# Layer 0's q, k and v of a two-layer masked-attention kernel: tokens stationary and 384 columns moving instead of 128

## Chip, cores and metric

The kernel runs on one core of a Trainium2 chip, in fp32 throughout. The time is the device time of one execution in microseconds (us); below it is the median of the runs shown. A profile is one further execution, recorded instruction by instruction. PE is TensorE (PEld its weight loads), DVE VectorE, ACT ScalarE, POOL GpSimd, and SP is the engine whose queue issues the DMAs here.

## What is computed

128 graphs of 128 nodes with 512 features each go through two layers of masked attention. Both layers use the same adjacency mask; layer 1 adds the diagonal to it. Cut to what matters (`norm` is a layer norm over the features, without gains unless named):

```python
def layer0(x):                                  # 4 heads of 64
    q, k, v = x @ Wq, x @ Wk, x @ Wv            # 512 -> 256 each
    sim = where(adj, q @ k.T * 64 ** -0.5, -max)
    return softmax(sim) @ v @ Wo + bo           # per head, then 256 -> 512
def layer1(x):                                  # 8 heads of 64
    q, k, v = split((norm(x) * gamma + beta) @ w_qkv.T)   # 512 -> 3 x 512
    sim = where(adj | eye, q @ k.T * 64 ** -0.5, -1e9)
    return softmax(sim) @ v @ w_out.T + b_out
x = norm(x + layer0(x)); x = norm(x + layer1(x))
```

## The kernel before

**Groups and steps.** Two graphs make a group, so there are 64 groups of 256 tokens. The kernel is a software pipeline written out by hand: `opening()` handles the first groups, `step(s)` runs for s from 2 to 63, and two closing functions and `last()` drain it. In one step layer 0's q, k, v are made for group s, layer 0's scores for group s - 1, layer 0's attention output for group s - 2, and layer 1 runs three to five groups behind. Nothing reorders the instructions: the order of the calls in `step` is the order of each engine's queue, and an engine that waits holds up everything behind it on its own queue. All DMAs go through SP's queue in the same way.

**Products.** Every large product (layer 0's q, k, v at L460, layer 1's q, k and v at L338, both output projections at L498) is made by a seven-product scheme on 2 x 2 blocks instead of eight. The two rows of blocks are the two graphs, the sums of blocks of the input (`xs`, `so`) are formed by POOL at L302, and those of the weights are formed once. Each of the seven products is taken out of PSUM by ACT or DVE (L469, L471, L474). A matmul holds one operand of 128 columns in the array (stationary) and streams the other (moving).

**Layer 0's products, the lines changed.** In `product_0` (L438) each of the seven products is six matmuls of 128 moving columns: for q and k the weights are stationary and the tokens move, so they come out with features on partitions, as the scores want them; for v the tokens are stationary. Two of the six belong to each of q, k and v, one for each half of that block's features. The three results lie side by side in one PSUM bank as 384 columns and are taken out together into `qkv0`. v's slot in `qkv0` alternates between the two ends with the group's parity, because the attention of group s - 2 is still to read it.

**x with features on partitions.** The products need x turned. Groups 0 to 2 are turned by PE (`transposed`, L239, matmuls L245, copies L246). Later groups go through DRAM: `load_ahead` loads x with tokens on partitions, `turn` has DVE transpose 32 x 32 blocks (L229) and writes them to a DRAM scratch (`put`, L214), `arrive` fetches them with the block rows moved to the right partitions in four DMAs of 32 partitions each (`fetch`, L220), and `in_order` has ACT copy them into place (L256). Layer 1's input, its q and k, and all probabilities go through DRAM in the same way, with the same helpers and the same scratch tile `turned` (two buffers).

**Order around the change.** `product_0(s, 4)` is followed by layer 1's q, k products; then come the third part's normalisation (DVE's reciprocal L588, POOL's multiplication L589), its block transposition (L607) and the fetch of the first two parts' probabilities. At the end of a step ACT orders layer 1's q (L412); the next step begins with the scores (L531 for layer 0, L536 for layer 1).

Of the kernel before, what the change touches and what calls it, by code (L numbers as in the profile page):

```python
# [10 lines left out]
F32 = mybir.dt.float32  # L11
# [6 lines left out]
P = 128  # L18
D = 64
G = 2  # L20
# [7 lines left out]
def kernel(ctx: ExitStack, tc: tile.TileContext, x, adj, wq, wk, wv, wo, bo,  # L28
# [45 lines left out]

    X = {}

# [10 lines left out]
    def load(g):  # L87
        load_rows(g)
        load_mask(g)

    def load_ahead(g):
        if g < NG:
            X[0] = one.tile([P, G, E], F32, tag="x", name=f"x_{g}")
            nc.sync.dma_start(X[0], x[g * G:(g + 1) * G].rearrange("b n e -> n b e"))
            load_mask(g)

    R[0] = five.tile([P, G, E], F32, tag="r", name="r_0")
    M[0] = six.tile([P, G, N], U8, tag="m", name="m_0")
    for b in range(G):
        nc.sync.dma_start(R[0][:, b], x[b])  # L100

# [9 lines left out]
    HF = INNER[0] // 2  # L111
    w0 = const.tile([P, KC, 2, 3, HF], F32, name="w0")
    ws0 = const.tile([P, 3, KC // 2, 3, HF], F32, name="ws0")
    for h in range(2):
        for i, w in enumerate((wq, wk, wv)):
            nc.sync.dma_start(w0[:, :, h, i, :], w[:, h * HF:(h + 1) * HF].rearrange("(c p) f -> p c f", p=P))
    nc.sync.dma_start(M[0], adj[:G].rearrange("b i j -> i b j"))
    load(1)
# [4 lines left out]
    bias1 = const.tile([P, E], F32, name="bias1")  # L123
    nc.sync.dma_start(bias1, b_out[None, :].to_broadcast([P, E]))

    w1 = const.tile([P, KC, 3 * INNER[1]], F32, name="w1")
# [60 lines left out]
    def weight_sums_0():  # L187
        combine(*(w0[:, c:c + KH, h].rearrange("p c t f -> p c (t f)") for c in (0, KH) for h in range(2)),
                *(ws0[:, i].rearrange("p c t f -> p c (t f)") for i in range(3)))

# [14 lines left out]
    WO = (wo0, wo1)  # L205
    RATIO, XT, V = {}, {}, {}
    qkv0 = const.tile([P, G, 2, 4, P], F32, name="qkv0")
# [3 lines left out]
    def put(t, name):  # L211

        scr = dram.tile(list(t.shape), F32, tag=name.split("_")[0], name=name)
        nc.sync.dma_start(scr, t)  # L214
        return scr
# [7 lines left out]

    def turn(l, g):
        if not 0 <= g < NG:
            return
        t = one.tile([P, 4, G * KC * 32], F32, tag="turned", bufs=2, name=f"turned{l}_{g}")
        for b in range(G):
            nc.vector.transpose(t.rearrange("p a (b c i) -> p a b c i", b=G, c=KC)[:, :, b],  # L229
                                (R[g] if l else X[0])[:, b].rearrange("p (c a i) -> p a c i", a=4, i=32))  # L230
        SCR[l] = put(t, f"scr{l}_{g}")

    def arrive(l, g):
        if not 0 <= g < NG:
            return
        RAW[l] = one.tile([P, 4, G, KC, 32], F32, tag=("raw0", "raw")[l], name=f"raw{l}_{g}")
        fetch(RAW[l].rearrange("p a b c i -> p a (b c i)"), SCR[l])

    def transposed(g):  # L239

        xT = XT[0, g] = one.tile([P, KC, T], F32, tag="xT0", name=f"xT0_{g}")
        for b in range(G):
            pt = mm_tile(f"xt{g}_{b}")
            for c in range(KC):
                nc.tensor.transpose(pt[:, c * N:(c + 1) * N], R[g][:, b, c * P:(c + 1) * P], ident)  # L245
            (nc.scalar.copy, nc.vector.tensor_copy)[b](xT[:, :, b * N:(b + 1) * N],  # L246
                                                       pt.rearrange("p (c n) -> p c n", c=KC))
        sums(0, g)

    def in_order(g):  # L250

        if not 0 <= g < NG:
            return
        xT = XT[0, g] = one.tile([P, KC, T], F32, tag="xT0", name=f"xT0_{g}")
        for b in range(G):
            nc.scalar.copy(xT[:, :, b * N:(b + 1) * N].rearrange("p c (a j) -> p a c j", a=4),  # L256
                           RAW[0][:, :, b])

# [108 lines left out]
    def taken_tokens(g, i, src):  # L367

        if i in (1, 5, 6):
            return tap("qk", g, i, src)  # L370
        if i == 4:
            done = src
        else:
            done = EV["qk", {2: 1, 3: 6, 7: 5}[i]]
            nc.vector.tensor_add(done, src, done)
        what, b = {2: ("k", 0), 7: ("q", 1), 3: ("q", 0), 4: ("k", 1)}[i]
        if i in (2, 7):
            TQ[what] = one.tile([P, 4, G, K1 * 32], F32, tag={"k": "xT0", "q": "raw"}[what],
                                name=f"t{what}_{g}")
            SCRQ[what] = dram.tile([P, 4, G, K1 * 32], F32, tag=f"scr{what}", name=f"scr{what}_{g}")  # L380
        t = TQ[what][:, :, b]
        nc.vector.transpose(t.rearrange("p q (c j) -> p q c j", j=32),
                            done.rearrange("p (c q j) -> p q c j", q=4, j=32))
        if what == "k":
            nc.sync.dma_start(SCRQ[what][:, :, b], t)
        elif i == 3:
            nc.sync.dma_start(SCRQ[what], TQ[what])
# [50 lines left out]
    def product_0(g, *which):  # L438
# [3 lines left out]
        xT = XT[0, g].rearrange("p (h c) (b n) -> p b h c n", h=2, b=2)  # L442
        xs = XS[0, g]
        for i in which:
            left = {1: xT[:, 0, 0], 2: xT[:, 0, 1], 3: xs[:, 3], 4: xT[:, 1, 1], 5: xs[:, 0],
                    6: xs[:, 1], 7: xs[:, 2]}[i]
            right = {1: w0[:, :KH, 0], 2: w0[:, KH:, 0], 3: w0[:, KH:, 1], 4: ws0[:, 2],
                     5: w0[:, :KH, 1], 6: ws0[:, 0], 7: ws0[:, 1]}[i]
            bank, first = INTO[i]
# [4 lines left out]
            acc = ACC[0, bank]  # L454
            odd = g % 2
            todo = [(t, c) for t in range(3) for c in range(KH)]
            for n, (t, c) in enumerate(todo):
                lhsT, rhs = (right[:, c, t], left[:, c]) if t < 2 else (left[:, c], right[:, c, t])
                at = (t + odd) % 3
                nc.tensor.matmul(acc[:, at * P:(at + 1) * P], lhsT, rhs, start=first and n == 0,  # L460
                                 stop=n == len(todo) - 1, skip_group_check=True)
            src = acc[:, :3 * P]
# [51 lines left out]
    def scores(s, *parts):  # L514

        made = {}
        for part in parts or PARTS:
# [8 lines left out]
            if part == 0:  # L526
                for b in range(G):
                    for h in range(HEADS[0]):
                        r = slice((h % 2) * D, (h % 2 + 1) * D)
                        q_, k_ = (qkv0[r, b, h // 2, i, :] for i in (1, 2))  # L530
                        nc.tensor.matmul(ps[h % 2][:, b * K0 + h // 2, :], q_, k_, start=True, stop=True)  # L531
            else:
                b = part - 1
                for h in range(HEADS[1]):
                    r = slice((h % 2) * D, (h % 2 + 1) * D)
                    nc.tensor.matmul(ps[h % 2][:, h // 2, :].rearrange("p (a j) -> p a j", j=32),  # L536
                                     QO[g, b][r, h // 2], keys_of(g, b, h // 2, r), start=True, stop=True)
# [245 lines left out]
    def opening():  # L783

        transposed(0)
        cleared(1, 0)

        for h in range(2):
            nc.scalar.activation(w0[:, :, h, 0, :], w0[:, :, h, 0, :], AF.Copy, scale=SCALE)
        product_0(0, 1)  # L790
# [6 lines left out]
        product_0(0, 4)  # L797
        transposed(1)

        made = scores(1)  # L800
# [17 lines left out]
        product_0(1, 4)  # L818
        transposed(2)

    def step(s):
# [3 lines left out]
        if s > 3:  # L825
            in_order(s)
            sums(0, s)
            arrive(1, s - 3)
        flush()
        load_rows(s - 1)  # L830
        masked(made, s, 0, 1, 2)
        if s == 3:
            turn(1, s - 3)
            arrive(1, s - 3)
        attend(s)
# [16 lines left out]
        stats(0, s - 2, 0)  # L852
        if s == 2:
            turn(0, s + 1)
            arrive(0, s + 1)
        product_0(s, 6)
# [14 lines left out]
        if s == 3:  # L871
            weight_sums(w1qk, wsqk, 1)
        if s > 2:
            turn(0, s + 1)
        product_0(s, 4)
        if s in (2, 3):
            prepare(len(setup) - (s == 2))
        normalised(s, 2)
        qk(s - 3, 1)
        if s == 2:  # L880
            prepare(1)
            in_order(s + 1)
        flush()
        if s > 2:
            probs_arrive(s, 0, 1)
        qk(s - 3, 2)
        blocks(s, 2)
        qk(s - 3, 6)
# [14 lines left out]
        probs_arrive(s, 2)  # L903
        if s > 2:
            arrive(0, s + 1)
        out_product(1, s - 5, 1, 2)
# [6 lines left out]
        if s > 2:  # L913
            turn(1, s - 2)
        cleared(s + 1, 0, 1, 2)
# [3 lines left out]
        out_product(1, s - 5, 7, 3, 4)  # L919
        q_in_order(s - 3)  # L920
        addend(0, s - 1)
        v(s - 3, 7)
# [6 lines left out]
        if s == NG - 1:  # L929
            arrive(1, s - 2)  # L930
            addend(1, s - 4)
# [186 lines left out]
```

## Time and profile before

| What | Value |
|---|---|
| Median of three runs (lowest to highest) | 2762.74 us (2762.73 to 2763.69) |
| The profiled execution's own time | 2765.02 us |
| Its span, first to last instruction | 2763.2 us |
| Granted PE clock, mean | 0.999 |
| PE matmul records | 18353, of which 5376 at L460 |
| DMA: bytes, mean rate | 561.42 MB, 203 GB/s |
| DMA packets' share of 16 engines | 72.0% |

The span leaves out what lies around the instructions, so it is a little under its own execution's time. In the profile's lines the parts are: line of the code, engine, operation, out<-in by the program's names, sizes; x gives the count, and in brackets stands the idle time before and what ended it. A matmul's duration there reaches from its start to the modelled end of its drain, and successive matmuls overlap. "SPq" is SP's queue issuing a DMA; the transfer itself goes on after it.

### The profile page before, as it was taken

The page shows a single profiled execution, that of the slowest core. Times are in us where ns is not written, and L with a number is a line of the kernel's source. Part 1 is how long each engine was busy: PE and PEld are TensorE (multiplying, and loading weights), DVE is VectorE, ACT ScalarE, POOL GpSimd, SP SyncE. Part 2 cuts the span into 40 slices and gives each one's busy share as a digit, 9 for nine tenths or more (in the row PEclk, how much of TensorE's full clock was granted, in tenths as well). Part 3 has the DMA queues.
Part 4 walks back from the last instruction along what each step waited for, and adds up shares of the span by engine and source line. Part 5 has one row for each costly group of instructions (what it writes and reads, how often), then busy time and mean ns, then how long its engine had stood idle before and what let it go on. Part 6 is the DMA issues. An engine that isn't in the chain of part 4 may idle for free.

```text
span 2763.2 us, 53794 instructions
## 1 busy us (share of the span) xinstructions
PE 2742.5 (99%) x18353; PEld 2180.1 (79%) x18353; DVE 1948.0 (70%) x3537; ACT 1526.8 (55%) x4869; POOL 1749.0 (63%) x2311
## 2 busy tenths in 40 slices
PE   9999999999999999999999999999999999999998
PEld 8978778778787787787777877877878778778787
DVE  5777677677677776776777767767767777677664
ACT  4456465465564564655655646546556455465554
POOL 5566666666666666666666666666666666666664
PEclk9999999999999999999999999999999999999999
DMA  5567877777778778777777787777777777877741
GB/s 171 154 201 208 222 209 210 215 209 213 215 208 219 209 206 227 206 211 213 209 221 207 206 224 207 210 216 208 215 214 208 217 211 207 223 208 212 196 118 62
DMA packets 473760, 561.42 MB, mean 203 GB/s; under 512 B 52104, under 2 KB 366992, under 8 KB 473488
## 3 DMA queue, kind: packets, MB, share of 16 engines
q1 hardware_dynamic: 473488, 557.99, 72.0%
q8 instruction: 147, 2.41, 0.4%
q14 instruction: 125, 1.02, 0.1%
HBM read 299.37 MB, written 258.47 MB: 202 GB/s over the span
## 4 chain that ended last, share of the span: by engine, by line
PE 97%; DMA 1%; POOL 1%; ACT 1%; DVE 1%; issue 0%; SPq 0%; POOLq 0%; ACTq 0%; DVEq 0%
PE qka L338 16%; PE a L460 13%; PE oa L498 12%; PE qkf L338 8%; PE va L338 8%; PE av L659 6%; PE f L460 6%; PE of L498 6%; PE qkc L338 4%; PE vf L338 4%; PE c L460 3%; PE oc L498 3%; PE sc L531 2%; PE sc L536 2%; PE vc L338 2%; PE sc_a L536 2%
## 5 line engine op out<-in xcount | busy, mean ns | idle before, releaser
L580 ACT ACTIVATE sm<-sm,nmax 128x128 f32<-128x128 f32 x1536 | 595.9, 395 | 7.0 <-DVE nmax L571 5.3
L589 POOL TENSOR_TENSOR sm<-sm,rec 128x1024 f32<-128x1024 f32 x192 | 364.1, 1896 | 292.9 <-DVE rec L588 292.9
L681 POOL TENSOR_TENSOR r<-r,bias 128x1024 f32<-128x1024 f32 x128 | 301.4, 2356 | 139.6 <-ACT r L680 139.6
L502 DVE TENSOR_TENSOR r<-oa,r 128x256 f32<-128x256 f32 x508 | 212.3, 418 | 170.1 <-PE oa L498 138.3
L580 ACT ACTIVATION_READ_ACCUMULATOR sm<-sm,nmax 128x1 f32 x1536 | 298.1, 194 | 0.0
L348 ACT COPY ev<-va 128x256 f32<-128x256 f32 x128 | 47.7, 372 | 438.3 <-PE va L338 438.2
L700 POOL TENSOR_SCALAR ve<-mv 128x2 f32<-128x2 f32 x191 | 41.4, 217 | 372.8 <-DVE mv L693 362.3
L607 DVE STREAM_TRANSPOSE turnedp<-sm 128x1024 f32<-128x1024 f32 x188 | 233.4, 1242 | 48.6 <-POOL sm L589 43.8
L302 POOL TENSOR_TENSOR xs<-xT 128x256 f32<-128x256 f32 x256 | 187.9, 734 | 111.0 <-ACT xT L256 91.1
L571 DVE TENSOR_REDUCE nmax<-sm 128x8 f32<-128x1024 f32 x192 | 226.2, 1203 | 0.1
L338 PE MATMUL qka<-wsqk,xs 128*128 128x512 f32 x472 | 221.8, 592 | 0.0
L338 PE MATMUL qkf<-w,xs 128*128 128x512 f32 x472 | 221.8, 592 | 0.0
L498 PE MATMUL oa<-wso,so 128*128 128x256 f32 x760 | 206.3, 380 | 2.1 <-POOL so L302 1.8
L498 PE MATMUL of<-wo,so 128*128 128x256 f32 x760 | 206.1, 380 | 0.8 <-POOL so L302 0.4
L726 ACT ACTIVATE r<-r,shift,root 128x512 f32<-128x512 f32 x254 | 192.6, 807 | 0.6 <-POOL shift L715 0.6
L565 DVE COPY_PREDICATED sm<-m,sc 128x512 f32<-128x512 uint8 x256 | 172.8, 728 | 12.2 <-PE sc L531 3.3
L338 PEld LDWEIGHTS qkf<-w,xs 128*128 128x128 f32 x472 | 89.7, 190 | 112.9 <-issue 112.9
L338 PEld LDWEIGHTS qka<-wsqk,xs 128*128 128x128 f32 x472 | 89.7, 190 | 112.9 <-issue 98.8
L692 DVE BATCH_NORM_STATS2 st<-r 128x6 f32<-128x512 f32 x254 | 174.9, 689 | 2.3
L551 POOL MEMSET sm<- 128x1024 f32 x192 | 174.9, 952 | 0.0
L498 PEld LDWEIGHTS of<-wo,so 128*128 128x128 f32 x760 | 143.7, 190 | 22.0 <-POOL so L302 2.1
L302 POOL TENSOR_TENSOR so<-aT 128x256 f32<-128x256 f32 (+1 forms) x254 | 150.5, 592 | 4.4 <-ACT aT L664 2.3
(182 smaller groups left out, 6788.7 us busy)
## 6 DMA issues: line engine op xcount, KB each, us to landing
scrp<-turnedp SPq DMA_DIRECT2D x188, 512.0 KB, 3.2
pT<-scrp SPq DMA_DIRECT2D x252, 256.0 KB, 4.8
scr<-turned SPq DMA_DIRECT2D x123, 512.0 KB, 3.0
raw<-scr SPq DMA_DIRECT2D x492, 128.0 KB, 3.9
r<-in_x_dram SPq DMA_DIRECT2D x63, 512.0 KB, 3.8
out_dram<-r SPq DMA_DIRECT2D x63, 512.0 KB, 3.5
pT<-scrp SPq DMA_DIRECT2D x248, 128.0 KB, 4.1
x<-in_x_dram SPq DMA_DIRECT2D x61, 512.0 KB, 5.8
```

Of the source, the lines that this page charges most:

```text
L302: nc.gpsimd.tensor_tensor(o, a0, a1, op=op)
L338: nc.tensor.matmul(o, lhsT, rhs, start=first and m == 0, stop=m == len(todo) - 1, skip_group_check=True)
L460: nc.tensor.matmul(acc[:, at * P:(at + 1) * P], lhsT, rhs, start=first and n == 0, stop=n == len(todo) - 1, skip_group_check=True)
L498: nc.tensor.matmul(acc, left[:, c], right[:, c], start=first and c == 0, stop=c == hk - 1, skip_group_check=True)
L502: nc.vector.tensor_add(part, acc, part)
L551: nc.gpsimd.memset(sm, NEG1 if part else NEG0)
L571: nc.vector.tensor_reduce(NMAX[part], SM[part], AX.X, ALU.max, negate=True)
L580: nc.scalar.activation(sm[:, i, k, :], sm[:, i, k, :], AF.Exp, bias=nmax[:, i, k:k + 1], accum_out=total[:, i, k:k + 1])
L589: nc.gpsimd.tensor_tensor(SM[part], SM[part], rec[:, :, :, None].to_broadcast([P, 2, K1, N]), op=ALU.mult)
L607: nc.vector.transpose(t.rearrange("p q (h r) -> p q h r", r=32), SM.pop(part).rearrange("p i k (q r) -> p q (i k) r", r=32))
L681: nc.gpsimd.tensor_tensor(R[g], R[g], (bias0, bias1)[l][:, None, :].to_broadcast([P, G, E]), op=ALU.add)
L726: nc.scalar.activation(R[g][:, b], R[g][:, b], AF.Identity, bias=shift[:, b:b + 1], scale=root[:, b:b + 1])
```

## The change

For groups from 3 on, the tokens are stationary for q and k too, and the weights of q, k and v move together: 384 columns in a matmul for even groups; for odd groups, where v lies at the other end, 256 for q and k and 128 for v. The weights' layout in `w0` changes so that q, k and v of one half are one access. q and k then come out with tokens on partitions, and are turned through DRAM (`turn_qk0`, `arrive_qk0`); the keys are read by the scores straight from the fetched tile, in pieces of 32, and q is put in order by one ACT copy (`q0_in_order`). Groups 0, 1 and 2 (`PLAIN_0`) keep the six narrow matmuls.

x is no longer turned through DRAM, nor by PE. `load_quarters` loads it so that features 128a to 128a + 127 of token 32m + j lie on partition 32a + j; one block transposition by DVE, in two instructions, then gives x with features on partitions. The features' order over the partitions changes with it, so the weights of layer 0 are loaded in the same order, in four DMAs each, those of wq from ACT's queue. x as rows is loaded separately for all groups. Layer 1's k gets a scratch tile of its own, one graph at a time, since it shared one with the turned x.

```diff
+    def load_quarters(g):
+        X[0] = one.tile([P, BB, E // 4], F32, tag="x", name=f"x_{g}")
+        src = x[g * G:(g + 1) * G].rearrange("b (m j) (a f) -> a j (b m) f", j=32, a=4)
+        for a in range(4):
+            nc.sync.dma_start(X[0][32 * a:32 * a + 32], src[a])
     def load_ahead(g):
         if g < NG:
-            X[0] = one.tile([P, G, E], F32, tag="x", name=f"x_{g}")
-            nc.sync.dma_start(X[0], x[g * G:(g + 1) * G].rearrange("b n e -> n b e"))
+            load_quarters(g)
             load_mask(g)
+    def transposed(g):
+        xT = XT[0, g] = one.tile([P, KC, T], F32, tag="xT0", name=f"xT0_{g}")
+        half = BB // 2
+        for m in (slice(0, half), slice(half, BB)):
+            nc.vector.transpose(xT.rearrange("p c (m j) -> p m c j", j=32)[:, m],
+                                X[0][:, m].rearrange("p m (c i) -> p m c i", i=32))
+    load_quarters(0)
...
-    w0 = const.tile([P, KC, 2, 3, HF], F32, name="w0")
+    w0 = const.tile([P, KC, 3, 2, HF], F32, name="w0")
-    for h in range(2):
-        for i, w in enumerate((wq, wk, wv)):
-            nc.sync.dma_start(w0[:, :, h, i, :], w[:, h * HF:(h + 1) * HF].rearrange("(c p) f -> p c f", p=P))
+    for i, w in enumerate((wq, wk, wv)):
+        for a in range(4):
+            (nc.sync if i else nc.scalar).dma_start(
+                w0[32 * a:32 * a + 32, :, i].rearrange("p c h f -> p c (h f)"),
+                w[a * P:(a + 1) * P].rearrange("(c i) f -> i c f", i=32))
+    load_mask(0)
+    load_rows(0)
     load(1)
...
+    transposed(0)
+    load_quarters(1)
...
+    def turn_qk0(g):
+        if not 0 <= g < NG or g in PLAIN_0:
+            return
+        t = one.tile([P, 4, 2, 4, 32], F32, tag="turned", bufs=2, name=f"turnedqk_{g}")
+        for i in range(2):
+            nc.vector.transpose(t[:, :, i], qkv0.rearrange("p b h t (q j) -> p q t (b h) j", j=32)[:, :, 1 + i])
+        SCR[0] = put(t.rearrange("p q t m j -> p q (t m j)"), f"scrqk_{g}")
+    def arrive_qk0(g):
+        if 0 <= g < NG and g not in PLAIN_0:
+            RAW[0] = one.tile([P, 4, 2, 4, 32], F32, tag="raw0", name=f"rawqk_{g}")
+            fetch(RAW[0].rearrange("p a t m j -> p a (t m j)"), SCR[0])
+    def q0_in_order(g):
+        if 0 <= g < NG and g not in PLAIN_0:
+            nc.scalar.copy(qkv0.rearrange("p b h t (a j) -> p t (b h) a j", j=32)[:, 1],
+                           RAW[0][:, :, 0].rearrange("p a m j -> p m a j"))
...
-            todo = [(t, c) for t in range(3) for c in range(KH)]
+            elif odd:
+                todo = [(parts[:, lo:hi], left[:, c], right[:, c, t0:t1])
+                        for lo, hi, t0, t1 in ((1, 3, 0, 2), (0, 1, 2, 3)) for c in range(KH)]
+            else:
+                todo = [(parts, left[:, c], right[:, c]) for c in range(KH)]
...
     def opening():
-        transposed(0)
+        sums(0, 0)
...
     def step(s):
         if s > 3:
-            in_order(s)
             sums(0, s)
-            arrive(1, s - 3)
+            arrive(s - 3)
...
-        if s > 2:
-            turn(0, s + 1)
         product_0(s, 4)
+        transposed(s + 1)
+        turn_qk0(s)
...
         qk(s - 3, 2)
+        arrive_qk0(s)
         blocks(s, 2)
...
         probs_arrive(s, 2)
-        if s > 2:
-            arrive(0, s + 1)
...
         q_in_order(s - 3)
+        q0_in_order(s)
```

In `opening`, `transposed(1)` is followed by `load_quarters(2)` and the sums; step 2's own calls of `turn(0, 3)`, `arrive(0, 3)` and `in_order(3)` are gone.

## The prediction

> **What bounds the kernel now.** I read the page's busy shares first, then the shares of the chain that ended last.
>
> ```profile
> PE 2742.5 (99%) x18353; PEld 2180.1 (79%) x18353; DVE 1948.0 (70%) x3537; ACT 1526.8 (55%) x4869; POOL 1749.0 (63%) x2311
> PE 97%; DMA 1%; POOL 1%; ACT 1%; DVE 1%; issue 0%; SPq 0%; POOLq 0%; ACTq 0%; DVEq 0%
> ```
>
> PE is both the busy engine and the path. A busy PE proves little by itself, so I looked for its gaps: between the scores of consecutive groups the trace has 42.35 us in 56 of the 58 steps from 5 to 62, and the chain in order of time is PE piece after piece without a hole. So the price of a matmul is its place in that chain, not the mean duration of its record (a 128-wide record lasts 275 ns, but the next starts after 112). Lines of the chain (start, length, piece), steady state and opening:
>
> ```profile
> 1237.80 1.34 PE c L460 x12
> 1239.13 0.43 PE oa L498 x2
> 1247.56 1.72 PE qka L338 x4
> ...
> 72.25 1.79 PE qka L338 x16
> ```
>
> Every fp32 matmul stands as two records ("passes"): the code asks for 42 x 64 = 2688 matmuls at L460, the trace has 5376 records. A pass moving 128 columns costs 1.34/12 = 111.6 ns (means of the starts: 111.5 to 111.7), 256 columns 215.8, 512 columns 1.717/4 = 429.2. The last two lie on a line, 0.8336 ns a column plus 2.4 ns; 128 lies 2.5 ns above it. The last line is a control in this kernel: the plain qk products of early groups do the same arithmetic in 16 narrow passes, 1.79 us where 4 wide ones take 1.72.
>
> **What the skill says.** "TensorE: Matmul & The Clock Gate", section "Back-to-back issue gap", lists 134, 262 and 518 cycles for N of 128, 256, 512: a constant per matmul, so wider is cheaper per column. This trace agrees in form (one fp32 pass takes twice the column time, then 2.4 ns, 4.9 at 128). "VectorE: DVE Perf Modes", section "The three transpose paths": the DVE transposes only 32x32 blocks. That is why a full turn needs a DRAM trip here, and why loading feature quarters onto partition quarters can spare it; a 128x512 block transpose takes 0.68 to 0.71 us in this trace. "DMA: Bandwidth & Descriptors", section "Issuing engines are not separate DMA queues": moving wq's loads to ACT saves issue time, not bandwidth. No run here shows loads issued by ACT yet.
>
> **The change, part by part.**
>
> *Products.* For groups 3 to 63 a product's 12 narrow passes become 4 of 384 columns (30 even groups), or 4 of 256 and 4 of 128 (31 odd ones, since v stays in the other slot). No row has 384 columns: the line gives 0.8336 x 384 + 2.4 = 322.5 ns; bounds are 320.0 (no constant) and 325.0 (the constant of 128), and at worst three narrow passes, 334.8. I take 322.5. Even: 7 x (12 x 111.6 - 4 x 322.5) = 7 x (1339 - 1290) = 0.344 us. Odd: 7 x (1339 - (863 + 446)) = 0.207 us. Sum 30 x 0.344 + 31 x 0.207 = 10.3 + 6.4 = **16.7 us**, all on the path; from 384 and from the odd narrow passes (109.1 on the line to 114) come -4.2 to +4.2. That w0 is now read in three pieces of 128 I cost at nothing: keys in four pieces of 32 (L536) go 16 passes in 0.89 us, and the same form takes over layer 0's scores, now L531.
>
> *x.* The turn of x through DRAM goes (2 transposes, 1 put, 4 fetches, 2 ACT copies of 0.617). In its place 4 loads of 128 KB, and 2 transposes of the same size, later by one product in DVE's order. *q, k.* Added: 2 DVE transposes (2 x 0.70), 1 put, 4 fetches, 1 ACT copy (0.62). Per step DVE +1.4 us, ACT -0.6, SP +3 issues; the sums of x on POOL no longer wait for ACT's copies at the step's start (91 us of POOL idle in all, none of it on the path). Where they land decides; DVE, ACT and SP at one step's handover:
>
> ```profile
> 1204.94 0.52 DVE L474 TENSOR_TENSOR qkv<-f,e 128x384 f32<-128x384 f32 x1
> 1205.38 1.28 DVE L229 STREAM_TRANSPOSE turned<-x 128x512 f32<-128x512 f32 x2
> 1206.59 0.16 DVE L588 RECIPROCAL rec<-total 128x8 f32<-128x8 f32 x1
> 1208.75 0.69 DVE L375 TENSOR_TENSOR eqk<-qkc,eqk 128x512 f32<-128x512 f32 x1 [2.00 <-PE qkc L338]
> ...
> 1206.37 0.46 ACT L471 COPY qkv<-a 128x384 f32<-128x384 f32 x1
> ...
> 1206.69 0.34 SPq L214 DMA_DIRECT2D scr<-turned  x1
> 1208.32 1.78 SPq L220 DMA_DIRECT2D pT<-scrp  x4
> 1210.21 0.52 SPq L385 DMA_DIRECT2D scrk<-tk  x1
> 1211.54 0.52 SPq L611 DMA_DIRECT2D scrp<-turnedp  x1
> ```
>
> New wait 1: x's transposes wait for product 4's reads of xT0, which end about 1205.3 (qk starts 1205.2): DVE comes free just then, cost nothing. New wait 2: the q, k transposes wait for ACT's copy of product 4, 1206.83; they end about 1208.3. Queued behind them on DVE are the reciprocal (1206.6 to about 1208.4) and the first qk addition, which waited 2.00 us for PE anyway. The reciprocal's reader on POOL started at 1208.34 behind sums: 0.2 us late, absorbed before its transposition at 1210.27. New wait 3: k's two halves now share one tile, so the second half's transposition (1217.27) waits for the first half's put, issued by 1210.6 and landed 3.4 later: 1214.0, cost nothing. **So the DVE's 2.0 us hole is the cover; without it 1.4 us a step would be exposed.**
>
> SP: the put moves from 1206.7 to 1208.4, the four pT fetches and the k put slip 0.4, and the new fetches wait for the put to land (3.0 us median), until 1211.4, and are issued by 1213.2. Behind them the third part's put slips from 1211.5 to 1213.2. SP then has nothing until 1217. Later it saves the x fetches (1.85 us) and pays three more x loads (1.2). In bandwidth the fetches move from the step's end into 1211 to 1217, where the engines are full; the free time there (1216.5 to 1217.7, 1220) takes all but some 0.8 us, so q's landing slips 0.8. ACT then runs q's copies at about 1225.2 and the new one by 1227.1; the next scores stand at 1229.2. Slack 2 us: cost nothing. x's 512-byte packets take 27 ns, 1024 a group, against 84 for 256 of 2 KB: 1.7 instead of 1.3 us of 16 engines, or 2.4 if loads to 32 partitions run as slowly as the fetches do (218 GB/s). Off the path.
>
> *Opening.* This is the only place where DMA is on the path:
>
> ```profile
> 4.74 5.33 DMA w<-in_L_gnn_Wv_dram
> 10.38 5.69 DMA raw_r<-in_L_gnn_w_qkv_dram
> 16.12 0.67 PE w_qkvt L144 x4
> 21.08 0.87 PE xt L245 x8
> 36.98 0.87 PE xt L245 x8
> ```
>
> PE waits at 16.1 for the first rows of w_qkv; the DMA engines are full from 2 to 28 us (298, then 364 GB/s). Ahead of these rows now come x of group 0 once more (as rows) and x of group 1 in quarters: 1 MB, at 300 to 364 GB/s 2.9 to 3.5 us; SP has 9 more issues ahead at about 0.5 us, 4.5 us, less the waits it had. Weights in wider packets give some back. I take +3.0 us (1 to 5). Back come PE's transposes for groups 1 and 2, 0.87 each; but they covered the scores' wait for ACT's copy of product 4, which then shows about 0.55: 0.3 each. Those of group 0 gave way to 1.4 us of DVE before the first product, inside the same wait for weights. Net **+2.4 us** (-0.5 to +5).
>
> **Sum.** 2763.2 (span; the profiled execution itself took 2765.02) - 16.7 + 2.4 = 2748.9. The median of the runs shown, 2762.74, is 0.5 under that span; the same difference gives 2748.4. I say **2748.5**.
>
> **Rivals.**
> 1. *Forecast*, chance 0.74: 2748.5, own range 2742 to 2755 (-4.2 and -2.9; +4.2 and +2.6).
> 2. *The opening gives instead of takes* (weights land sooner in wider packets, rows are not waited for), 0.08: -16.7 - 3 or more, about 2742.
> 3. *Width pays nothing at 384* (three pieces cost three passes, 334.8): even groups 0, odd 6.4, opening +2.4: 2758.7. Against it speaks the line through 256 and 512. Chance 0.05; or a stall of some 0.2 us a step with the same result, 0.02.
> 4. *A small stall in every step*, some 0.1 us from DVE's fuller handover: 61 x 0.1 = 6.1, 2754.6. Chance 0.05.
> 5. *Slower*: q's way through DRAM becomes the bound. The copy of layer 0's q stands on ACT behind layer 1's q copies (1.15), which wait for fetches queued behind all new traffic; scores of the next step, first on PE, wait for it. For it: those fetches were already just in time (ACT waited for them in 12 of 59 groups), and DMA is full there. Against it: slack. It decides once q's landing slips over 2.6 us instead of 0.8; at 3.4 us each step stalls 0.8, 61 x 0.8 = 49, less 14: about 2797. Chance 0.06.
>
> **Numbers.** A change within 0.2% (5.5 us) cannot be told from none. Faster: cases 1, 2, 4, 0.87; same: case 3, 0.07; slower: case 5, 0.06. Range 2741 to 2757: it takes in both bounds of the 384-wide pass and of the opening, cases 2 and 4.
>
> **What would show it.** Right: steps of 42.01 us (even) and 42.14 us (odd) where 42.35 stood; L460 pieces of 1.29 and 1.31 us; no L245; the first w_qkvt near 19 us; DVE near 72%, its wait for qkc gone from 2.0 to some 0.3. Wrong: PE idle before L531 with ACT's q copy or a DMA as its releaser (case 5), PE waiting for a bank that DVE reads late at the qk products (case 4), 384-wide passes near 335 (case 3).

## The result, and the profile after

| | median, us | lowest to highest | ratio to before (95% interval) |
|---|---|---|---|
| before, 12 runs | 2762.93 | 2762.37 to 2764.33 | |
| changed, 12 runs | 2763.99 | 2759.03 to 2765.92 | 1.0003 (0.9994 to 1.0012) |

No difference that can be measured; the forecast was 14 us faster. The changed kernel's times also spread over 6.9 us where the other's spread over 2.0. Its profiled execution was its fastest, 2759.03 us (span 2757.3), so a second one was profiled as well (own time 2764.44, span 2762.7), which is nearer to the median. The busy shares and the shares of the chain that ended last, in the first:

```profile
PE 2725.2 (99%) x15781; PEld 2024.6 (73%) x15781; DVE 2025.0 (73%) x3662; ACT 1510.6 (55%) x4805; POOL 1750.2 (63%) x2311
PE 89%; DMA 4%; ACT 3%; DVE 1%; POOL 1%; SPq 1%; issue 1%; ACTq 0%; POOLq 0%; DVEq 0%
```

PE is as busy in share as before, but its part of the chain fell from 97% to 89%: 11% of the path now runs through other things, DMA first. In the second execution it is 84%, with 6% DMA. What the matmuls themselves did is read from the chain (start, length, piece), group s odd, then even:

```profile
1238.07 1.31 PE c L490 x8
...
1280.19 1.29 PE c L490 x4
```

These answer to 1.34 us for 12 narrow passes before, and are the 1.31 and 1.29 that were forecast. Steps that nothing disturbs take 42.00 us (even) and 42.14 us (odd) where 42.35 stood. So the width pays in full; the time is lost elsewhere. Three lines of the list of waits (engine and line waiting, what for: us in total, times, longest) lead there:

```profile
ACT qo L435 <- DMA rawq<-scrq: 133.8, 59, 3.6
DVE eqk L396 <- PE qkc L359: 20.2, 59, 0.4
DVE tk L405 <- DMA scrk<-tk: 19.4, 22, 1.7
```

The middle one is DVE's hole in every step, 115.6 us in all before and now 20.2: it is filled by the new transpositions, as costed. The other two are DMAs. ACT's wait for layer 1's fetched q was 4.1 us in 12 steps before and is now in every step; DVE's wait at the k transposition for its own previous put did not exist. One step in the chain in order of time (step 13) shows the second of these at work:

```profile
490.49 1.30 DVE turnedqk L267 x2
...
491.88 0.28 SPq L234
...
494.57 7.34 DMA scrk<-tk
...
502.00 0.73 DVE tk L405
...
502.78 1.13 PE va L359 x4
```

The new transpositions (L267) and the issue of the new put (L234) stand ahead on the chain. The put of k's first half is issued at 494.57 and lands 7.34 us later. Only then may DVE overwrite the tile with the second half (it had been free for 1.51 us by then), and PE's product `va`, which needs the bank that DVE was to empty, starts 0.32 us late. SP's queue in the same step (start, length of the issue):

```profile
492.33 2.14 SPq L240 DMA_DIRECT2D pT<-scrp  x4
494.57 0.52 SPq L408 DMA_DIRECT2D scrk<-tk  x1
495.13 2.16 SPq L240 DMA_DIRECT2D rawqk<-scrqk  x4
497.74 0.52 SPq L643 DMA_DIRECT2D scrp<-turnedp  x1
500.52 0.34 SPq L410 DMA_DIRECT2D scrq<-tq  x1
502.75 0.52 SPq L408 DMA_DIRECT2D scrk<-tk  x1
506.09 1.73 SPq L240 DMA_DIRECT2D rawq<-scrq  x4
```

The k put is issued right behind a fetch of four DMAs that stood there before as well. The new fetch of four more follows it, and the q put comes behind that. The fetch of q, which waits for its put, follows 5.6 us after the put's issue.

**Where the time went.** Steps are counted from one group's layer 0 scores to the next. Against a second profile of the kernel before (own time 2763.11, span 2761.3; the experiments tell why not the first), the second profile of the changed one gives:

| Stretch | Forecast, us | Measured, us |
|---|---|---|
| Width: steps 5 to 62 at 42.00 and 42.14 instead of 42.35 | -16.0 | -16.4 |
| What these steps take above 42.00 and 42.14 | 0 | +11.4 |
| Opening, up to the scores of step 5 | +1.85 | +4.5 |
| Last step before the closing | -0.2 | +0.2 |
| Closing, from the last layer 0 scores to the end | 0 | +1.65 |
| Sum | -14.3 | +1.4 |

The forecast's 16.7 us of width were for 61 steps. 58 of them have 16.0; those of steps 3 and 4 (0.55) are taken off the opening's +2.4 here, that of step 63 (0.2) stands in the last step. The spans differ by 1.4 too. In the first profile of the changed kernel the second line is 6.5 us: the stalls are what varies from execution to execution. Set side by side, the steps of one profile lose time on PE at two places only: at the products `va` and `vc` 4.9 us in the first profile and 6.8 in the second, in 10 or 11 steps, and at the next step's scores and the product right behind them 1.7 and 4.6.

### The profile page after: what moved, and what is told of

The parts are those of the page before. It is cut to its first block, busy times and chain, and to the rows that moved or that the text cites. A ratio compares the mean times of both kernels' runs of the same rounds, so it can differ in the third digit from the quotient of the medians.

```text
span 2757.3 us, 49223 instructions
## 1 busy us (share of the span) xinstructions
PE 2725.2 (99%) x15781; PEld 2024.6 (73%) x15781; DVE 2025.0 (73%) x3662; ACT 1510.6 (55%) x4805; POOL 1750.2 (63%) x2311
## 4 chain that ended last, share of the span: by engine, by line
PE 89%; DMA 4%; ACT 3%; DVE 1%; POOL 1%; SPq 1%; issue 1%; ACTq 0%; POOLq 0%; DVEq 0%
PE qka L359 14%; PE a L490 11%; PE oa L528 11%; PE va L359 8%; PE qkf L359 7%; PE av L691 6%; PE of L528 6%; PE f L490 5%; PE vf L359 4%; PE qkc L359 4%; PE c L490 3%; PE oc L528 3%; PE sc L562 2%; PE sc L568 2%; PE vc L359 2%; DMA scrk<-tk 2%
## 5 line engine op out<-in xcount | busy, mean ns | idle before, releaser
L490 PE MATMUL a<-ws,xs 128*128 128x128 f32 (+1 forms) x760 | 182.1, 375 | 0.0
L490 PE MATMUL f<-w,xs 128*128 128x128 f32 (+1 forms) x760 | 182.1, 375 | 0.0
```

The costliest lines, as they stand in the source:

```text
L490: nc.tensor.matmul(o, lhsT, rhs, start=first and n == 0, stop=n == len(todo) - 1, skip_group_check=True)
```

## The experiments

**1. The two stalls of the steps.** First theory: the shared k tile makes DVE wait. Rival: the traffic is the matter, and the wait is only where it shows. The edit gives each half its own tile, from a pool that has free space:

```diff
-            TQ[what] = one.tile([P, 4, K1 * 32], F32, tag="tk", name=f"tk{b}_{g}")
+            TQ[what] = one.tile([P, 4, K1 * 32], F32, tag=f"qo{b}", name=f"tk{b}_{g}")
```

> The changed kernel, but layer 1's two k halves are turned in two tiles (they borrow the tiles of layer 1's ordered q, free at that time), so that the second transposition does not wait for the first half's put. Theory A, the one tile is the stall: the 19.4 us of DVE waiting on that put and PE's waits for DVE's transposition go, and in the timed runs 6 to 11 us with them: 2753 to 2758. Theory B, the DMA queue is simply late and the tile only where it shows first: the wait moves on to ACT's q copies and the scores behind them, 2761 to 2764.

Measured 2758.87 us, ratio 0.9986 (0.998 to 0.9993), 5.1 below the changed kernel's 2763.99 and between the two theories. DVE's wait is gone, but 5.7 us of stalls stay in the steps, and layer 0's scores wait for ACT's copy of the fetched q (L277), 12.3 us in 25 steps at the weight load and 3.2 in seven at the matmul. (Some 0.3 us of each of the 25 is no loss: the weight load has that gap in the other steps too.) So the tile is about half, and a second stall sits behind it: ACT's copy for layer 0 stands behind its copies of layer 1's q, which wait for the fetch. To take that away, the new fetch is issued later, behind layer 1's q and second k puts:

```diff
         qk(s - 3, 2)
-        arrive_qk0(s)
         blocks(s, 2)
...
         qk(s - 3, 3, 4)
+        arrive_qk0(s)
```

> As the run with two k tiles, and the fetch of layer 0's q and k is issued after the second k put instead of ahead of the third part's put. Theory A: nothing is left to gain, the same time as with two tiles within 1 us. Theory B: the third part's put, q's put and so q's fetch land some 2 us earlier, the scores stop waiting for ACT: 2751 to 2754, and ACT's 134 us of waiting for q's fetch fall to under 60.

Measured 2753.31 us, 0.9965 (0.9953 to 0.9978). The stalls of steps 5 to 62 are 1.0 us in all, and the scores' waits for ACT shrink to 1.7 us in four steps at the weight load and 0.3 in one at the matmul. One expectation missed: ACT's wait for layer 1's q.

```profile
ACT qo L435 <- DMA rawq<-scrq: 115.2, 59, 3.4
```

It fell only from 150.3 (with two tiles) to 115.2. The wait is not itself the loss; what mattered is when it ends. The q put, which landed after 5.0 us (median of the steps) in the changed kernel and 2.7 before, lands after 2.8 here. The same later fetch alone, with the k tile still shared:

> The changed kernel with its one k tile, with the fetch of layer 0's q and k after the second k put. If the tile's wait and the late fetch of q are two separate stalls of some 5 us each, as the first two runs say, only the second goes: 2757 to 2760, with DVE still waiting for the first k put. If the first stall was only a part of the second, 2753 to 2754.

Measured 2757.48 us, 0.9979 (0.9971 to 0.9987): 6.5 below the changed kernel. DVE's wait for its put stays, 19.6 us in 22 steps, and the scores' wait nearly goes. This run also tells whether the new fetch makes the k put late. In step 13, shown above, the fetch is now gone from behind the put, and the chain has:

```profile
493.25 7.15 DMA scrk<-tk
```

7.15 us instead of 7.34. Over the steps the put of k's first half lands after a median of 6.0 us here, 6.1 in the changed kernel and 5.8 before. So the new fetch right behind it is not what makes this put late. In steps 12, 13, 22, 23, 32, 33, 52 and 53 it takes 6.7 to 7.5 us in both kernels; why in these stays open.

The four kernels (changed, and these three) make a square: the second tile gives 5.1 without and 4.2 with the later fetch, the later fetch 6.5 without and 5.6 with the second tile. **Two stalls of some 5 and 6 us, nearly independent.**

**2. Is the width worth what it was said to be?** The turned products are kept and the matmuls made narrow again:

```diff
-            elif odd:
-                todo = [(parts[:, lo:hi], left[:, c], right[:, c, t0:t1])
-                        for lo, hi, t0, t1 in ((1, 3, 0, 2), (0, 1, 2, 3)) for c in range(KH)]
             else:
-                todo = [(parts, left[:, c], right[:, c]) for c in range(KH)]
+                todo = [(parts[:, (t + odd) % 3], left[:, c], right[:, c, t])
+                        for t in range(3) for c in range(KH)]
```

> The changed kernel with tokens stationary as it is, but q, k and v of a product as six matmuls of 128 moving columns again; everything else stays. If the wide matmuls save what the prediction priced, PE has 16.7 us more: 2780 if the stalls stay as they are, 2770 to 2775 if the longer step gives the late DMAs their time back. If the width saves nothing on the path, 2764.

Measured 2781.08 us, 1.0065 (1.0053 to 1.0078), 17.1 above the changed kernel; the 12 passes take 1.34 us again in the chain. The forecast had 16.7. Steps that nothing disturbs stand at 42.35 again, so 16.3 us of steps 5 to 62 are the width. That the whole comes so near to the forecast is in part luck, as in its profile the stalls (8.8 us) and the closing (133.7 us, 2.4 to 2.9 more) differ too. Against the kernel before, this run gives the price of the rest of the change when nothing is gained for it: 18 us.

**3. x's part alone.** All groups keep the six narrow matmuls with q and k coming out turned; x, the weights and the opening are as in the changed kernel.

```diff
-    PLAIN_0 = (0, 1, 2)
+    PLAIN_0 = range(64)
```

> The changed kernel with the old six matmuls for all groups, so no q, k through DRAM: the part on x alone (feature quarters, one block turn, weights in quarters). Theory A and B: only the opening is late, 4 to 5 us, no stalls in the steps: 2766 to 2768. Rival C, the quarter loads' small packets hold up the steps: over 2772.

Measured 2767.96 us, 1.0019 (1.0011 to 1.0027), 5.0 above before. Every step from 5 to 62 is 42.35, so x's way in quarters costs nothing in the steady state; the opening takes 4.9 more, and that is all of it. The stalls of the steps come from q and k. A run from the other side leaves out x's loads from group 3 on, in the changed kernel (x stays that of group 2, so the values are not those of the reference):

```diff
         if g < NG:
-            load_quarters(g)
             load_mask(g)
```

> The changed kernel (one k tile, early fetch) without the loads of x in quarters in the steps: groups 3 to 63 are computed from group 2's x, so the values are not the reference's; nothing else differs. Theory F, x's small packets make the DMA engines late for k's and q's puts: the stalls shrink, 2755 to 2759. Theory G, x's loads at the step's start are over long before the contested stretch and the puts are late because of what stands just ahead of them on the queue (the new put and 1 MB of probabilities): no change, 2761 to 2765.

Measured 2764.22 us, 1.0005 (0.9996 to 1.0013). Without these loads, DVE waits for its k put 38 times, 33.8 us. So x's traffic is not what makes the put late.

**4. The opening.** What the chain of the changed kernel shows:

```profile
1.66 5.27 DMA w<-in_L_gnn_Wq_dram
...
7.30 4.40 DMA w<-in_L_gnn_Wv_dram
...
17.99 4.05 DMA raw_r<-in_L_gnn_w_qkv_dram
22.04 0.04 issue
22.08 0.66 PE w_qkvt L165 x4
```

The first rows of w_qkv are waited for at 22.08 instead of 16.12, and they are asked for at 17.99 only, after a bias load of 6.25 us on which SP's queue was held: here each load's issue waits until the eighth load before it has landed, and for these rows that is the bias, issued at 11.72. And the first product, at 10.07 instead of 6.36, waits for ACT's scaling of wq, and through it for the weights in quarters. Their rate, by stretches of 2 us (the last column is GB/s, the one before it the DMA share):

```profile
4.00:6.00 2.00, 0.00 (x0) 0.00 (x0) 0.00 (x0) 0.00 (x0) 0.00 (x0) 1.00 1.18 200
6.00:8.00 2.00, 0.00 (x0) 0.00 (x0) 0.00 (x0) 0.00 (x0) 0.00 (x0) 1.00 1.15 201
```

200 GB/s with the DMA engines full, where before had 297 and 304 in the same stretches. Two remedies, on top of the two tiles and the later fetch. One has the first x and the weights loaded by two queues, partitions 0 to 63 from SP's, 64 to 127 from ACT's:

```diff
-    def load_quarters(g):
+    def load_quarters(g, halves=False):
...
-            nc.sync.dma_start(X[0][32 * a:32 * a + 32], src[a])
+            (nc.scalar if halves and a > 1 else nc.sync).dma_start(X[0][32 * a:32 * a + 32], src[a])
...
-    load_quarters(0)
+    load_quarters(0, True)
...
-            (nc.sync if i else nc.scalar).dma_start(
+            (nc.sync if a < 2 else nc.scalar).dma_start(
```

> The kernel with two k tiles and the later fetch (2753.3 us), with the opening's quarter loads of x and of the three weights issued from two queues at once: the first two quarters from SP, the last two from ACT. Theory D, the opening is late because each quarter load feeds 32 partitions only and they follow one another (209 to 217 GB/s where whole tiles had 298): the first product starts near 7.5 us instead of 10.0, and 2 to 3 us go: 2750 to 2751.5. Theory E, the opening is late because of the bytes put ahead of the w_qkv rows: PE starts earlier but waits for these rows just the same, under 1 us gained: 2752.5 to 2753.5.

Measured 2754.16 us, 0.9968 (0.9956 to 0.998): nothing gained over 2753.31. The rate did rise, to 263 and 253 GB/s in these two stretches, and the first scores stood at 25.37 instead of 26.58; but PE's wait for the rows of w_qkv grew from 1.59 to 2.16 us, and the profiled execution, the fastest of six, was not like the rest. The other remedy asks for the first four blocks of w_qkv rows right after the first mask, ahead of x's rows, wo and the biases:

```diff
+    early = [spare.pop(0) for _ in range(4)]
+    for r, raw in enumerate(early):
+        nc.sync.dma_start(raw, w_qkv[r * P:(r + 1) * P, :])
...
-    load_transposed(w1, w_qkv, "w_qkv")
+    load_transposed(w1, w_qkv, "w_qkv", early)
```

> The kernel with two k tiles and the later fetch, with the first four row blocks of w_qkv loaded straight after the weights of layer 0, ahead of x as rows, the biases and group 1's x. Theory D: only PE's wait for these rows, 1.6 us, goes: 2751.7. Theory E: the whole delay of the opening goes, 4 us: 2749.5.

Measured 2751.66 us, 0.9959 (0.9946 to 0.9971): 1.6 us gained, PE no longer waits for the rows. Both together:

> The kernel with two k tiles and the later fetch, with both changes of the opening. Theory D: the two add up, 4 us: 2749 to 2750. Theory E: as with the rows first alone, 2749.5. Both theories: the first w_qkv transposition stands near 17 us instead of 21.7.

Measured **2750.16 us, 0.9953 (0.994 to 0.9965)**, the best version here. Its chain at the start:

```profile
1.68 4.24 DMA w<-in_L_gnn_Wq_dram
...
5.94 3.37 DMA w<-in_L_gnn_Wv_dram
9.30 2.91 PE a L493 x12
...
18.98 0.87 PE w_qkvt L168 x8
```

From 9.30 on PE works without a hole up to the first scores; the first w_qkv transposition stands at 18.98, where 17 was expected. The two queues pay once the rows are no longer the next thing waited for, 1.5 us (medians of five runs each, whose ranges overlap; in the profiles the first scores stand at 23.38 instead of 25.98); the step 5 scores stand 1.1 us later than before instead of 4.5. A last idea on the opening concerned ACT (its work there, in the changed kernel):

```profile
8.10 1.28 ACT L821 ACT_TABLE_LOAD   x1 [8.10 <-DMA w<-in_L_gnn_Wq_dram]
9.39 1.15 ACT L821 ACTIVATE w<-w 128x512 f32<-128x512 f32 x2
```

The table load now stands behind the wait for wq's loads, and the scaling of wq behind the table load; before, it ran at 0.72 us while nothing was due. "ScalarE: Activation LUTs", section "What ACT_TABLE_LOAD costs", gives 1283 ns and a drain of about 1380 ns besides for a switch to another set; the trace has the 1.28 us, and the next instruction starts at once, so at this first load no drain shows. The edit puts a tiny activation between wq's loads and those of wk:

```diff
+        if i == 0:
+            first = const.tile([P, 4], F32, name="first")
+            nc.gpsimd.memset(first, 0.0)
+            nc.scalar.activation(first, first, AF.Copy, scale=SCALE)
```

> The kernel with two k tiles, the later fetch and both changes of the opening (2750.2 us), with one tiny ACT activation placed right after wq's loads, so that ACT's table load (1.28 us), which stood behind ACT's last DMA issues and ahead of wq's scaling, is over before. If it is on the opening's path, the first product starts 1.2 us earlier (8.1 instead of 9.3) and the time is 2749.0; if wk's and wv's landing sets the pace there, 2750.2.

Measured 2751.44 us, 0.9958 (0.9944 to 0.9972): 1.3 above the kernel without it (five runs each, and the ranges overlap again). The table load moved to 2.67 us, but ACT also issues half the loads of wk and wv, which came later for it, and the first full product then waited for these. In the kernel without it the first product, at 9.29, is released by wv's landing and not by ACT. So the landing of the weights sets the pace there, not the table.

**5. What is left over.** The changed kernel once more, for an execution near its median:

> The changed kernel once more, for a second profile: the first one was of its fastest execution, 5 us under its median. Both stall theories: the same opening, and some 6 to 12 us of stalls over the steps, at the same two places (DVE waiting for the first k put, the scores waiting for ACT's copy of layer 0's q).

Own time 2764.44: stalls of 11.4 us in the steps instead of 6.5, an opening of 4.5 as in the first. DVE's wait for its put is 27.5 us in 32 steps, the scores' for ACT's copy 9.0 in 17. And the kernel before once more:

> The kernel before, unchanged, profiled once more, to see what its closing (last scores of layer 0 to the end) takes in a second execution: the first had 131.36 us there at an own time of 2765.02, 2.1 above the median of the timed runs, while the x part alone, which has the same closing, had 129.55. If the closing is 129.5 here too at an own time near 2763, the changed kernel loses some 1.5 us in its closing as well, beside the opening and the stalls; if it is near 131.4 again, the closing costs nothing, and the 2.1 us are a difference between executions. Steps should stand at 42.35 with no stall worth over 2 us in all, and the first scores near 21.9 us.

Own time 2763.11, closing 129.69 us. The first profile's 131.36 had one piece that no other run has, the probabilities' product after the closing's longest wait, at 3.38 us instead of 1.97. That is 1.4 of the 1.7 us by which its closing is longer than this one and that of x's part alone (129.6). So the changed kernel's closing (130.86 and 131.34) is a loss; no kernel that turns q and k has less than 130.5 there. It lies at its start (PE and ACT, changed kernel, second profile):

```profile
2635.86 2.32 PE L359 MATMUL qka<-xT,w 128*128 128x128 f32 x16 [1.38 <-ACT xT L289]
```

```profile
2635.21 1.09 ACT L289 ACTIVATE xT<-raw,gb 128x256 f32<-128x256 f32 x2 [4.84 <-DMA raw<-scr]
```

Layer 1's turned x for a late group comes 1.4 us late, since its fetch was issued 1.5 us before the last layer 0 scores and took SP 2.92 us; in the kernel before it was issued 3.9 us ahead of them, in 1.73. The best version still has this wait (1.08). x's part alone does not, so it belongs to q and k too. No kernel here removes it, so this cause is read from the traces and not tested.

## Why the prediction was wrong, step by step

**Right.** The price of a 384-wide pass (322.5 ns on a line through 256 and 512; four of them take 1.29 us) and its sum: -16.0 forecast for steps 5 to 62, -16.4 measured. Reading w0 in three pieces costs nothing. DVE's hole covers the new transpositions: its wait for qkc went to 0.34 us a step, forecast 0.3; DVE stands at 73%. New waits 1 and 2 make PE wait nowhere by themselves; what they do to the k put follows. x's 512-byte packets are off the path.

**The step that failed first is New wait 3.** It has the put of k's first half "landed 3.4 later: 1214.0, cost nothing". 3.4 us was the median over all k puts. They are of two kinds, and the trace of before, asked for the one put that the new wait concerns, says so (the two halves of one step, each in a window of its own):

```profile
L385 SPq DMA_DIRECT2D scrk<-tk x1: 519/519/519, 1210.2 to 1210.2; - x1
...
DMA to landing us min/median/max: 5.6/5.6/5.6
```

```profile
L385 SPq DMA_DIRECT2D scrk<-tk x1: 513/513/513, 1218.0 to 1218.0; - x1
...
DMA to landing us min/median/max: 2.6/2.6/2.6
```

The first half's put, issued right behind four fetches, already took 5.6 us, the second's 2.6; over all steps of that trace the medians are 5.8 and 2.6. With 5.6 it lands at 1216.2 and the slack before 1217.27 is 1.1 us, not 3.3. The change uses that up. The put goes out 0.6 us later in its step (23.9 us after layer 0's scores, 23.3 before; 0.4 was forecast), behind the new put on SP's queue, which waits for the new transpositions. It takes a median of 6.1 us instead of 5.8. And DVE is ready for the second half 0.2 to 0.35 us earlier in the step. So DVE waits in 22 to 32 of 59 steps, and where the put takes about 7 us PE waits too. Worth 4 to 5 us, as the second tile shows; that the new fetch behind the put has no part in it, the run with one tile and the later fetch shows.

**The second is the slip of q's landing, 0.8.** It was estimated from free time in the DMA engines. The q put's landing alone went from 2.7 to 5.0 us, 2.3 more, as the new fetches were issued ahead of it, and is 2.8 again when they are issued later. ACT's first copy of layer 1's q starts 2.1 to 2.3 us later in its step in the median (39.7 and 39.9 us after layer 0's scores in the two profiles, 37.55 before), and 3.4 to 3.8 at most. This is the mechanism of rival 5, which was to decide from 2.6. In the median the slip stays under that, and ACT's copy for layer 0 ends about 1 us ahead of the scores; in 5 and 9 of 57 steps it ends less than 0.1 us ahead, and there the scores wait. So the cost, by the runs with the later fetch, is 5.6 to 6.5 us instead of 49. Rival 4 had the right size for one such stall (6.1), and its sign, PE waiting for a bank that DVE empties late, is in the trace, though at `va` and not at the qk products. But what holds DVE is a put, and not the work it has taken over.

**The third is the opening: +4.9 where +2.4 was taken** with a bound of 5. (+4.9 is x's part alone; the +4.5 of the changed kernel has the width of steps 3 and 4 in it.) Its mechanism, more bytes ahead of w_qkv's rows, holds: asking for the rows first brings 1.6. The term that was missing is the start of the first product, 3.7 us later, which the forecast had inside "the same wait for weights". The slower rate of loads to 32 partitions was seen in the fetches (218 GB/s) and used only for the steady state; in the opening all weights and x came at 200 GB/s.

**Not foreseen:** the closing, +1.65, where by the traces SP's later queue delays a fetch that had been in time.

All four go one way. By the table's lines, -14.3 with +11.4 for the stalls, +2.65 for the opening, +0.4 for the last step and +1.65 for the closing, less the 0.4 by which the width pays more than forecast, gives the +1.4 measured.

## What to carry to other kernels

When a change makes one instruction wait for a DMA, look up how long that very DMA takes at its place in the queue, not the median of its kind: a put behind four fetches took twice what a put of the same size took elsewhere in the step, and that stood in the trace of before. A turn through DRAM that is hidden by slack still lengthens the landing of whatever is issued after it, so fetch late, behind the puts that others wait for, and give each put in flight its own tile; here two short edits took the stalls of the steps from 11.4 us to 1.0. In the opening the order of the loads is the order of the work, and a load that is not full in partitions needs to be counted at its own rate.

## What the hardware showed that was not expected

- Loads of 128 KB to 32 partitions each, with the DMA engines full, ran at 200 to 214 GB/s (4 to 12 us) with wq's from one queue and the others from another; with each weight's quarters divided over the two queues by partition half, 253 to 263, and loads of whole tiles 297 to 304. "DMA: Bandwidth & Descriptors", section "Rules for kernel authors", says that two transfers to disjoint partition halves serialize and that more issuing queues bring no bandwidth. For these quarters the measurement differs. Whether the queues or the partition halves do it was not separated.
- A put of 256 KB (half of k) takes 2.6 us to land where only q's put is just ahead of it, and a median of 5.8 (5.5 to 7.1) right behind a fetch of 1 MB in four parts. A further fetch of 0.5 MB right behind the put makes no difference that shows: a median of 6.1 with it, 6.0 with it issued later.
- A stall by DMA varies between executions of one kernel: 6.5 and 11.4 us in two profiles. The kernel whose puts have slack, the best version, spread over 2.3 us (five runs), the changed one over 6.9 (twelve).
